# Attention's steps spread further, fill tokens found earlier, and three more tiles turned by transfers, in a fused attention and mixture-of-experts kernel

## Chip, cores, metric

One core of a Trainium2 chip. The time is device microseconds of one execution. The engines are TensorE (PE in the profile, with its weight loads PEld), VectorE (DVE), ScalarE (ACT), GpSimd (POOL) and SyncE (SP), which here only issues transfers.

## What is computed

The input is x, 8 sequences of 1024 tokens with 256 features. Everything is float32.

```python
xn = layernorm(x)
# causal linear attention, 16 heads of 16
q, k, v = xn @ Wq.T, xn @ Wk.T, xn @ Wv.T          # split into heads
q, k = elu(q) + 1, elu(k) + 1
out = einsum('blhd,blhde->blhe', q, cumsum(einsum('blhd,blhe->blhde', k, v), 1))
den = clip(einsum('blhd,blhd->blh', q, cumsum(k, 1)), 1e-6)
attn = (out / den).reshape(...) @ Wo.T
# mixture of 8 experts, the best 2 of each token
w, e = top_k(xn @ Wr + br, 2);  w = softmax(w)
ffn = sum over the 2 experts of w * ((silu(xn @ W1[e]) * (xn @ W3[e])) @ W2[e])
return x + attn + ffn
```

W1 and W3 are 256x512 for each expert, W2 is 512x256.

## The kernel before

**Two streams of work.** The 8192 tokens are 16 blocks of 512 for norm, router and attention. For the experts, each token appears twice; the 16,384 entries are sorted by expert and cut into rows of 128, called tiles here. There are room for 135 tiles (NF), of which 132 (NM) always run and 3 only if the counts ask for them. A first batch of 25 tiles (N1) comes from the first 4 blocks, so that expert work can begin early; a second list covers the rest and serves tiles 25 and up. `tile_step(j)` runs for j = 0 to 132: it carries tile j through the experts and puts beside it a piece of the other work: blocks 4 to 15 through norm, turn and router (j below 12), the making of the second list (j = 12 to 22, LISTS = 12, READ = 22), and steps of attention.

**A tile.** `ffn_load(j)` has POOL gather the tile's 128 rows of x (`xg`) and its entries of a small table (`entry`: router weight and the two numbers of the norm). `ffn_norm` (ACT) normalises the rows. PE needs them with features on partitions. Up to tile TURNED - 1 `ffn_turn` does that: two 128x128 transposes on PE into PSUM and a copy on ACT, all in step j - 1. From TURNED on, a transfer does it: `ffn_halves` (DVE) splits the float32 words into two planes of 16 bits, `ffn_turn_halves` has SP issue a transposing transfer between the loads of the tile's W1 and W3, and `ffn_join` (ACT) puts the planes together again in step j - 1. For this the norm comes in step j - 2, a step earlier than for a tile turned on PE. `ffn_hidden` makes gate and up (64 matmuls for the two, in `gu_ps`), silu on ACT and the product on DVE (`hT`); `ffn_out`, a step later, makes y (`y_ps`), scaled by the router weight on DVE; `ffn_store` has POOL add the rows to `out` (tiles 0 to 24: to a copy `acc_d`) with an indirect, adding transfer. Transfers that add to the same tensor wait for each other.

**Weights.** `ffn_weights(j + 2)` in step j has SP load 512 KB each of W1 and W3 into five buffers, so a load goes out when the matmuls five loads earlier are done. W2 stays resident.

**Attention's steps.** A block has 8 (`block_steps`): k, q, v; then scores of the first chunk, denominators (`den`, `over`) and their spreading over partitions by 8 transfers on SP (`rden`), and a load of the next block's turned x (`xnT`); then four chunks (`weigh` makes `oT`, `attend` multiplies by Wo into `a_ps` and copies to `at`), whose results POOL adds to `out` 256 KB at a time; the last block's go in one transfer of 512 KB (`n = NCH if t == NBLK - 1`). There are 129 steps (LAST), the last being only the final `attend`. `attend_upto` runs them up to a number `upto` that depends on j; 18 (AHEAD) are done after step 21.

**The second list.** `second_batch` is a generator, advanced by `piece(place)` at five places of a step, in steps 14 to 21 and once more at the start of step 22, and once at the end of step 12. Its first part computes counts and offsets; then 32 groups of one-hot matmuls (`held_ps`, from `at_place` on DVE and `parts` on ACT) add up, in `all_held`, which entry sits in each place. From that come `num_i` (which table row), `src_i` (which token to read) and `dst_i` (to which to add). Empty places must add their zeros to a token that no other row of the tile names; `other_tokens` finds one for each expert and partition (`fill`): a product `at_0_ps` on PE and nine operations on 128x8 elements on DVE. Then 15 operations on 128x110 turn `fill` into `fills`, place by place.

**What sets the order.** PE runs in program order. On the other engines a planner lays out the instructions at build time, in order of readiness and program order; those marked `in_order` are kept in place to a degree. Each engine then works through its queue in order.

The lines the change and the prediction touch: 764 to 787 (`second_batch`), 532 to 545 (`other_tokens`), 1476 (`TURNED`), 1523 (`piece`), 1584 (`upto`), 1312 to 1400 (a tile's load, halves, turns, weights), 1430 to 1447 (`ffn_out`, `ffn_store`), 1098 to 1117 (`attend`).

Of the kernel before, what the change touches and what calls it, by code (L numbers as in the profile page):

```python
# [64 lines left out]
def tile_attention_moe(  # L65
# [33 lines left out]
    NM = NF - NR  # L99
# [70 lines left out]
    for t in range(FB, FB + 2):  # L170
# [9 lines left out]
        fill=0.0, base=0, channel_multiplier=-1,  # L180
# [5 lines left out]
        fill=0.0, base=-1, channel_multiplier=-1,  # L186
# [8 lines left out]
        fill=0.0, base=0, channel_multiplier=1,  # L195
# [3 lines left out]
        fill=0.0, base=HD - 1, channel_multiplier=-1,  # L199
# [542 lines left out]
    def second_batch(taken):  # L742

        rows = sizes(True)
        left = f_one.tile([P, E], F32, name="left")
        nc.vector.tensor_tensor(left, rows, taken, ALU.subtract)
        upto = add_up(left, "upto2")
        past = past_experts(upto, N2, f_x, "xb")
        te, te_i = numbers_of(past, N2, "2")
        nc.vector.tensor_copy(rows_left, upto[0:1, E - 1 : E])  # L750

        room = f_one.tile([P, E - 1], F32, name="room2")
        nc.vector.tensor_scalar(
            room, rows[:, 0 : E - 1], -1.0, float(ROWS), ALU.mult, ALU.add
        )
        nc.vector.tensor_tensor(room, room, taken[:, 1:E], ALU.add)
        of_tiles = rows_of(past, past, room, taken[:, 0:1], N2, "rows2")
        in_row, place = places(NT)

        short = f_one.tile([P, E], F32, name="short")  # L760
        nc.vector.tensor_scalar(short, rows, 1.5, None, ALU.is_lt)
        num_i = const.tile([P, N2], I32, name="of2_i")
        all_held = f_one.tile([P, N2], F32, name="all_held")
        others = other_tokens(short)
        next(others)
        yield
        for j in range(2):
            for a in range(0, NT, 16):
                ps = ps_y.tile([P, 2, N2], F32, tag="y", name="held_ps")
                for b in range(a, a + 16, PART):  # L770
                    at, parts = one_hot(in_row, place, of_tiles, j, b, N2)
                    yield
                    for i in range(PART):
                        nc.tensor.matmul(
                            ps.rearrange("p w n -> p (w n)"), lhsT=at[:, i, :],
                            rhs=parts[:, i].rearrange("p w n -> p (w n)"),
                            start=(b + i == a), stop=(b + i == a + 15),
                        )
                for w in range(2):
                    if j == 0 and a == 0 and w == 0:  # L780
                        nc.vector.tensor_copy(all_held, ps[:, 0, :])
                    else:
                        nc.vector.tensor_tensor(all_held, ps[:, w, :], all_held, ALU.add)
                yield
        nc.vector.tensor_copy(num_i, all_held)
        _, src_i = tokens(all_held, N2, NT, "2_i")
        fill = next(others)
        fills = f_one.tile([P, N2], F32, name="fills")
        for e in range(E):
            mine = fills  # L790
            if e > 0:
                mine = f_two.tile([P, N2], F32, tag="mine", name="mine")
            nc.vector.tensor_scalar(
                mine, te, float(e), fill[:, e : e + 1], ALU.is_equal, ALU.mult
            )
            if e > 0:
                nc.vector.tensor_tensor(fills, fills, mine, ALU.add)
        empty = f_one.tile([P, N2], F32, tag="at_i", name="empty")
        nc.vector.tensor_scalar(empty, all_held, 0.5, None, ALU.is_lt)
        nc.vector.tensor_tensor(empty, empty, fills, ALU.mult)  # L800
        dst_i = const.tile([P, N2], I32, name="dst2_i")
        nc.vector.tensor_tensor(dst_i, src_i, empty, ALU.add)
        batches[1] = tab_d[1], te_i, num_i, src_i, out_rows, dst_i
        yield
# [346 lines left out]
    LAST = NBLK * STEPS + 1  # L1151
# [233 lines left out]
    def ffn_weights(j, halved=True):  # L1385
        e = expert_of(j, mybir.EngineType.SP)
        for s, w in enumerate((w1, w3)):
# [6 lines left out]
            )  # L1394
            if s == 0 and halved and j >= TURNED:
                ffn_turn_halves(j)
# [54 lines left out]
    def ffn_step(j, behind, between, after, late, finish):  # L1451
# [7 lines left out]
        if j < NM:  # L1459
            ffn_hidden(j, j == NM - 1, between)  # L1460
            after()
        if j + 1 < TURNED:
            ffn_turn(j + 1)
# [9 lines left out]
                stored[0] += 1  # L1473


    TURNED = 27
    gathered = ffn_load(0)
    with tc.issue_after(gathered.ins):
        in_order(nc.gpsimd.tensor_copy(te_late, batches[0][1]))
# [17 lines left out]
    LISTS = NBLK - FB  # L1497
    READ = LISTS + 10
    AHEAD = 2 + LISTS // 2 + READ - LISTS
# [12 lines left out]
    def tile_step(j):  # L1512
        nonlocal routing
        if j + 1 < TURNED:
            ffn_norm(j + 1)
        if TURNED <= j + 2 < NM:
            ffn_norm(j + 2)
            ffn_halves(j + 2)
        t = FB + j
        turning = 0 < j and t < NBLK  # L1520
        counting = FB < t <= NBLK and t % ROUND == 0

        def piece(place):
            if LISTS + 2 <= j < READ or (j, place) == (READ, 0):
                next(held["lists"])

        def of_routing():
            nonlocal routing
            if t <= NBLK:
                with tc.issue_after((last_token if j < 3 else last_masked)[0].ins):  # L1530
                    if "lgT" in held:
                        tp = ps_y.tile([P, P], F32, tag="y", name="lg_t")
                        nc.tensor.transpose(tp, held.pop("lgT"), ident)
                        add_logits(t - 1, 1, tp)
                    if routing and not counting:
                        for _ in routing:
                            pass
                        routing = None
                    if counting:
                        routing = route(t - ROUND, t)  # L1540
                        next(routing)
                    of_blocks = [] if j == 0 else [t + 1, t + 2] if j == 1 else [t + 2]
                    if not counting:
                        take_stats(of_blocks)

        def between():
            if not stepped and j > 0:
                of_routing()
            if turning:
                turn(t)  # L1550
            piece(2)

        def after():
            piece(3)

        def late():
            nonlocal waits
            if waits:
                attend_upto(waits)
                waits = None  # L1560

        def finish():
            if turning:
                held["lgT"] = f_two.tile([P, P], F32, tag="lgT", name="lgT")
                nc.scalar.copy(held["lgT"], logits(t))
            if counting:
                next(routing)
                with tc.issue_after(held_y[0].ins):
                    take_stats([t + 2])
            if t + 1 < NBLK:  # L1570
                normalise(t + 1)
            if turning and t + 5 < NBLK:
                load_x(t + 5, nc.scalar)

        if LISTS <= j < LISTS + NBLK - FB:
            rows = slice((t - LISTS) * TB, (t - LISTS + 1) * TB)
            in_order(nc.sync.dma_start(out=out_rows[rows, :], in_=x_rows[rows, :]))
        piece(0)
        if j < LISTS:
            upto = 3 + j // 2  # L1580
        elif j < READ:
            upto = AHEAD - (READ - j - 1)
        else:
            upto = AHEAD + (LAST - AHEAD) * (j - READ + 1) // (NM - 3 - READ)
        before_step = steps_made[0]
        waits = attend_upto(upto, put_off=True)
        stepped = steps_made[0] > before_step
        if stepped or j == 0:
            of_routing()
        piece(1)  # L1590
        ffn_step(j, LATE if N1 < j <= N1 + LATE else 0, between, after, late, finish)
        piece(4)
        if j == LISTS:
            for _ in routing:
                pass
            in_order(
                nc.sync.dma_start(
                    out=tab_d[1][1 : 1 + NS * P, :].rearrange("(p i) w -> p (i w)", p=P),
                    in_=tab.rearrange("p i w -> p (i w)"),
                )  # L1600
            )
            in_order(nc.sync.dma_start(out=tab_d[1][0:1, :], in_=before[0:1, 0:3]))
            held["lists"] = second_batch(taken)
            next(held["lists"])
        if j == N1 + 1:
            copied.append(j)
            in_order(nc.sync.dma_start(out=out_rows[0 : FT * P, :], in_=acc_d[:, :]))

    routing = None
    with tc.manual_schedule(engines={EN.PE}):  # L1610
        for j in range(NM + 1):
            tile_step(j)
# [54 lines left out]
```

## Time and profile before

Three runs took 1238.14, 1243.5 and 1246.43 us, median 1243.5. The profiled execution took 1239.72 us, its span (first to last instruction) 1238.0, at a mean granted clock of 0.995.

| | PE | PE weight load | DVE | ACT | POOL |
|---|---|---|---|---|---|
| busy us | 1193.1 | 1051.0 | 689.0 | 588.9 | 551.1 |
| share of the span | 96% | 85% | 56% | 48% | 45% |

| stage | us | PE busy | DMA share |
|---|---|---|---|
| first blocks, first list | 0 to 62 | 47.02 of 62 | 0.93 |
| second list, from tile 13 on | 155 to 279 | 118.97 of 124 | 0.66 |
| middle | 400 to 600 | 198.48 of 200 | 0.92 |
| middle | 800 to 1000 | 199.16 of 200 | 0.94 |
| last tiles | 1195 to 1225 | 28.23 of 30 | 0.65 |
| after PE | 1225 to 1238 | 0 | 0.18 |

The DMA share is the mean busy share of the 16 DMA engines. In a row of the timeline stand: start, duration, engine and line, operation, output and inputs with their shapes, how many in a row were merged, and in brackets how long the engine had been idle before and what ended that (the releaser, inferred from semaphores). SPq is SP's queue, where the duration is that of issuing, not of the transfer.

### The profile page before, as it was taken

To read this page: it belongs to the slowest core of one execution; us is meant where nothing else is said; L and a number is where in the kernel's file an instruction comes from. 1 tells how busy PE (TensorE), PEld (TensorE's weight loads), DVE (VectorE), ACT (ScalarE), POOL (GpSimd) and SP (SyncE) were. 2 spreads that over 40 slices of the span, in tenths; PEclk is the share of its full clock that TensorE was granted. 3 is DMA by queue.
4 is the path that set the end of the run, shared out by engine and by line. 5 is a ranking of instruction groups with operands and counts; after the bars stand their busy time and mean duration, and the time that the engine had idled before them with its cause. 6 is when DMAs were issued, how large, how long until landed. Compare 5 with 4: busy or idle time off the path is not lost. (4 is left out here: it accounts for less than half of the span.)

```text
span 1238.0 us, 29843 instructions
## 1 busy us (share of the span) xinstructions
PE 1193.1 (96%) x11394; PEld 1051.0 (85%) x11394; DVE 689.0 (56%) x1519; ACT 588.9 (48%) x1098; POOL 551.1 (45%) x473
## 2 busy tenths in 40 slices
PE   8799999999999999999999999999999999999995
PEld 6588887977889888989888898889898888889884
DVE  7766678765464545546464645454554646464541
ACT  5656576771543526262624445352627262534521
POOL 4734434334353645353455444454444544454422
PEclk9999999999999999999999999999999999999998
DMA  9888777657979899989999898899999988999884
GB/s 330 291 270 282 197 201 204 202 154 194 244 182 213 185 224 192 206 188 206 188 198 196 188 218 183 190 200 222 191 212 187 222 170 207 189 195 211 183 180 71
DMA packets 232446, 252.67 MB, mean 204 GB/s; under 512 B 101458, under 2 KB 156370, under 8 KB 232018
## 3 DMA queue, kind: packets, MB, share of 16 engines
q1 hardware_dynamic: 189298, 198.61, 58.8%
q0 software_dynamic: 38256, 43.22, 25.2%
q10 hardware_dynamic: 4752, 8.91, 2.0%
q8 instruction: 94, 1.54, 0.5%
q14 instruction: 46, 0.38, 0.1%
HBM read 187.91 MB, written 44.29 MB: 188 GB/s over the span
## 5 line engine op out<-in xcount | busy, mean ns | idle before, releaser
L1411 PE MATMUL gu_ps<-xgT,w 128*128 128x128 f32 x4224 | 506.2, 277 | 5.9 <-issue 3.0
L1411 PEld LDWEIGHTS gu_ps<-xgT,w 128*128 128x128 f32 x4224 | 490.6, 192 | 20.7 <-issue 12.0
L1443 POOL DMA_INDIRECT out_dram<-y,dst_i x107 | 175.6, 1641 | 330.6 <-DVE y L1437 52.8
L1430 PE MATMUL y_ps<-w_sb,hT 128*128 x1056 | 250.4, 380 | 1.3 <-DVE hT L1422 0.9
L1419 ACT ACTIVATE hT<-gu_ps 128x512 f32<-128x512 f32 x132 | 79.4, 602 | 291.4 <-PE gu_ps L1411 245.4
L1430 PEld LDWEIGHTS y_ps<-w_sb,hT 128*128 128x128 f32 x1056 | 190.5, 190 | 22.9 <-issue 1.2
L1025 DVE TENSOR_TENSOR s_sb<-s_ps,causal 128x512 f32<-128x512 f32 x256 | 162.0, 685 | 85.3 <-PE s_ps L1016 72.7
L1315 POOL DMA_INDIRECT xg<-in_x_dram,src_i x132 | 135.6, 1027 | 148.9 <-DVE half L1340 49.7
L1320 POOL DMA_INDIRECT entry<-tab_d,of_i x107 | 109.9, 1027 | 32.6 <-issue 32.0
L1422 DVE TENSOR_TENSOR hT<-gu_ps,hT 128x512 f32<-128x512 f32 x132 | 90.5, 685 | 48.5 <-PE gu_ps L1411 28.9
L1437 DVE TENSOR_SCALAR y<-y_ps,entry 128x256 f32<-128x256 f32 x132 | 63.6, 481 | 94.7 <-PE y_ps L1430 86.8
L1340 DVE COPY half<-xg 128x512 uint16<-128x512 uint16 x105 | 47.9, 456 | 109.0 <-ACT xg L1330 99.7
L1114 ACT COPY at<-a_ps 128x256 f32<-128x256 f32 x64 | 23.8, 371 | 173.0 <-PE a_ps L1109 156.8
L1358 ACT COPY xgT<-halfT 128x512 uint16<-128x512 uint16 x105 | 80.3, 765 | 3.5 <-DMA halfT<-half 1.9
L1330 ACT ACTIVATE xg<-xg,entry 128x256 f32<-128x256 f32 x132 | 79.0, 599 | 2.8 <-DMA xg<-in_x_dram,src_i 2.6
L1016 PE MATMUL s_ps<-qm,kT 32*128 32x256 f32 x1024 | 74.4, 400 | 0.6 <-DVE hT L1422 0.6
L1109 PE MATMUL a_ps<-wo_sb,oT 128*128 128x256 f32 x256 | 67.8, 387 | 4.9 <-DVE oT L1080 4.9
L1443 POOL DMA_INDIRECT acc_d<-y,src_i x25 | 42.7, 1709 | 65.0 <-DVE y L1437 20.0
L1063 PE MATMUL o_ps<-s_sb,va 128*32 128x128 f32 x2048 | 69.7, 276 | 0.2 <-issue 0.2
L1063 PEld LDWEIGHTS o_ps<-s_sb,va 128*32 128x32 f32 x2048 | 52.3, 109 | 18.3 <-issue 16.4
L1117 POOL DMA_DIRECT2D out_dram<-at x26 | 34.7, 1336 | 68.8 <-DMA out_dram<-y,dst_i 42.2
L1016 PEld LDWEIGHTS s_ps<-qm,kT 32*128 32x128 f32 x1024 | 47.0, 184 | 14.6 <-issue 7.4
(236 smaller groups left out, 1418.4 us busy)
## 6 DMA issues: line engine op xcount, KB each, us to landing
w<-in_w_dram SPq DMA_DIRECT2D x264, 512.0 KB
rden<-over SPq DMA_DIRECT2D x128, 64.0 KB
xnT<-xnT_d SPq DMA_DIRECT2D x15, 512.0 KB
out_dram<-at POOLq DMA_DIRECT2D x25, 256.0 KB
out_dram<-in_x_dram SPq DMA_DIRECT2D x12, 512.0 KB
xnT_d<-xnT ACTq DMA_DIRECT2D x11, 512.0 KB
xb<-in_x_dram SPq DMA_DIRECT2D x9, 512.0 KB
w_sb<-in_w_dram SPq DMA_DIRECT2D x4, 1024.0 KB
```

The lines of the kernel that those rows point to most:

```text
L1016: nc.tensor.matmul(s_ps[r][:, hh].rearrange("p a l -> p (a l)"), lhsT=kT[rows, hh, span], rhs=qm[rows, hh, :, span], start=True, stop=True,)
L1025: last_masked[0] = nc.vector.tensor_tensor(sm, s_ps[r].rearrange("p k a l -> p (k a) l"), causal_b, ALU.mult)
L1063: nc.tensor.matmul(o_ps[32 * r : 32 * r + 32, hh, :], lhsT=va[:, c, 4 * hh + r, a, :], rhs=s_sb[r][:, 2 * hh + a, :], start=(first and a = ...
L1315: rows = nc.gpsimd.indirect_dma_start(out=xg[j], out_offset=None, in_=x_rows[:, :], in_offset=bass.IndirectOffsetOnAxis(ap=src_i[:, i : i ...
L1320: of_rows = nc.gpsimd.indirect_dma_start(out=entry[j], out_offset=None, in_=table[:, :], in_offset=bass.IndirectOffsetOnAxis(ap=num_i[:, i ...
L1330: nc.scalar.activation(xg[j], xg[j], AF.Identity, bias=entry[j][:, 1:2], scale=entry[j][:, 2:3])
L1358: nc.scalar.copy(xgT[j].bitcast(U16).rearrange("p k (l b) -> p b k l", b=2), halves.pop(j).rearrange("p (b k) l -> p b k l", b=2),)
L1411: done = nc.tensor.matmul(ps[:, i, :], lhsT=w13[:, k, bass.ts(i, P)], rhs=xgT[j][:, k, :], start=(k == 0), stop=(k == KC - 1),)
L1419: silu = nc.scalar.activation(hT, gu[0], AF.Silu)
L1422: nc.vector.tensor_tensor(hT, gu[1], hT, ALU.mult)
L1430: done = nc.tensor.matmul(y_ps, lhsT=hT[:, i, :], rhs=w2_sb[:, bass.ds(e * (IC * H) + i * H, H)], start=(i == 0), stop=(i == IC - 1),)
L1443: nc.gpsimd.indirect_dma_start(out=rows[:, :], out_offset=bass.IndirectOffsetOnAxis(ap=dst_i[:, i : i + 1], axis=0), in_=ys.pop(j), in_off ...
```

## The change

Three edits.

1. Attention's steps after READ are spread so that the last come in step 130, not 128. (The words of the change speak of one last transfer; that it is one is so in the kernel before already.)
2. In `second_batch`, `fill` is asked for after its own new stop, in step 13 (`piece(1)`, after attention's step and ahead of the tile's gate and up matmuls), instead of behind the list in step 22. What turns it into `fills` stays.
3. TURNED goes from 27 to 24: the rows of tiles 24, 25 and 26 are turned by transfers.

```diff
         others = other_tokens(short)
         next(others)
         yield
+        fill = next(others)
+        yield
         for j in range(2):
...
         nc.vector.tensor_copy(num_i, all_held)
         _, src_i = tokens(all_held, N2, NT, "2_i")
-        fill = next(others)
         fills = f_one.tile([P, N2], F32, name="fills")
...
-    TURNED = 27
+    TURNED = 24
...
         def piece(place):
-            if LISTS + 2 <= j < READ or (j, place) == (READ, 0):
+            if LISTS + 2 <= j < READ or (j, place) in ((READ, 0), (LISTS + 1, 1)):
                 next(held["lists"])
...
-            upto = AHEAD + (LAST - AHEAD) * (j - READ + 1) // (NM - 3 - READ)
+            upto = AHEAD + (LAST - AHEAD) * (j - READ + 1) // (NM - 1 - READ)
```

## The prediction

> **What bounds the kernel now.** I read the share of busy time by stretches first, then the chain that ended last, then the timeline of the last 70 us and of 260 to 310 us, where the edits land.
>
> ```profile
> 600.00:800.00 200.00, 198.38 (x1904) 175.62 (x1903) 105.50 (x190) 89.07 (x146) 94.45 (x76) 1.00 0.92 199
> ...
> 1205.00:1215.00 10.00, 10.00 (x79) 9.67 (x78) 1.97 (x5) 2.50 (x4) 1.65 (x1) 1.00 1.00 205
> 1215.00:1225.00 10.00, 8.86 (x56) 7.72 (x54) 2.54 (x5) 0.60 (x1) 3.10 (x2) 1.00 0.31 36
> ```
>
> The columns are stretch, length, busy us of PE, weight load, DVE, ACT and POOL, granted clock, DMA share, GB/s. PE works 99% of the middle at full clock; no step of attention there waits for a free slot. So moving attention's steps between tiles can't shorten the middle. Only less PE work, a stall, or the end can change the time. The end is not PE's:
>
> ```profile
> 1197.42 1.56 POOL L1443 DMA_INDIRECT out_dram<-y,dst_i  x1 [7.44 <-DVE y L1437]
> 1201.76 1.40 POOL L1117 DMA_DIRECT2D out_dram<-at  x1 [2.78 <-ACT at L1114]
> 1212.07 1.65 POOL L1443 DMA_INDIRECT out_dram<-y,dst_i  x1 [8.92 <-DVE y L1437]
> 1216.68 1.55 POOL L1443 DMA_INDIRECT out_dram<-y,dst_i  x1 [2.96 <-issue]
> 1221.26 1.54 POOL L1443 DMA_INDIRECT out_dram<-y,dst_i  x1 [3.02 <-DVE y L1437]
> 1226.59 1.55 POOL L1443 DMA_INDIRECT out_dram<-y,dst_i  x1 [3.79 <-DVEq L1621]
> 1231.05 1.54 POOL L1443 DMA_INDIRECT out_dram<-y,dst_i  x1 [2.91 <-DMA out_dram<-y,dst_i]
> ```
>
> The stores of tiles 126 to 131, with attention's last transfer (512 KB) between the first two. All add to `out`, so each goes out when the one before has landed. The releaser in the third row is wrong: tile 127's y was there at 1206.49 (its DVE row: 1206.01 + 0.48), so it was the transfer that held the store back, 10.31 us after its own issue. From there four steps of 4.6, 4.6, 5.3 and 4.5 us lead to the last store, though PE ends at 1224.71 and tile 131's y at 1225.23. The end, 1238.0, is 6.95 us behind the last store's issue. The queue of stores is 5.8 us late (1231.05 against 1225.23).
>
> **The turns by transfer.** Three pairs like
>
> ```profile
> 285.10 0.38 PE L1368 MATMUL xg_t<-ident,xg 128*128 128x128 f32 x2
> ```
>
> leave PE: 3 x 0.38 = -1.14 us, all on the path, as PE is full. For it come three half copies on DVE (0.43 to 0.76), on ACT copies of 0.76 for 0.37, and three transposes on SP's queue (1.25 each). Norms of tiles 24 to 26 come a tile earlier. Tile 24's rows were asked for at 242.24, tile 25's at 274.32, just ahead of its norm at about 277; ACT then idles up to 281.72 (4.20 us), so a wait of a microsecond there is covered. With that cover gone it would cost that microsecond. The tight place is tile 25's transpose, because of SP's order:
>
> ```profile
> 284.23 7.09 SPq L997 DMA_DIRECT2D rden<-over  x8
> 291.36 0.67 SPq L830 DMA_DIRECT2D xnT<-xnT_d  x1
> 292.83 4.14 SPq L1390 DMA_DIRECT2D w<-in_w_dram  x5
> 297.10 1.64 SPq L1349 DMA_TRANSPOSE halfT<-half  x1
> ```
>
> The five loads are both of tiles 25 and 26 and the first of 27 (the row below them is tile 27's transpose). Tile 25's transpose would stand behind the first, at 293.3. What one takes in this traffic, a later place tells:
>
> ```profile
> 506.43 1.26 SPq L1349 DMA_TRANSPOSE halfT<-half  x1
> ...
> 513.85 0.77 ACT L1358 COPY xgT<-halfT 128x512 uint16<-128x512 uint16 x1 [0.58 <-DMA halfT<-half]
> ```
>
> 7.4 us to use; two other joins that waited give 7.0 (707.85 to 714.88) and 6.8 (1040.70 to 1047.47). So tile 25's join starts at 300.1 to 300.7 and ends 0.76 later. PE, rid of two turns, reaches its gate/up matmuls (300.79 now) at 300.03: a stall of 0.8 to 1.5, taken as 1.1. The other order: from block 3 on, where such transposes exist, SP has the loads and the transpose of the next tile but one ahead of rden (349.71 and 357.27 against 357.71). Then tile 25's goes out at about 279, nothing waits, and part of this stall of 1.38 us may go:
>
> ```profile
> 294.89 0.76 DVE L1340 COPY half<-xg 128x512 uint16<-128x512 uint16 x1 [0.91 <-ACT xg L1330]
> 295.57 0.47 DVE L1437 TENSOR_SCALAR y<-y_ps,entry 128x256 f32<-128x256 f32 x1
> 295.96 0.41 DVE L1080 TENSOR_TENSOR oT<-rden,o_ps 128x256 f32<-128x256 f32 x1
> 296.24 0.99 POOL L1320 DMA_INDIRECT entry<-tab_d,of_i  x1 [0.30 <-issue]
> ...
> 296.51 1.10 PE L1109 MATMUL a_ps<-wo_sb,oT 128*128 128x256 f32 x4 [1.38 <-DVE oT L1080]
> ```
>
> oT stands behind tile 27's half copy, which waits for a double norm that this change moves to tile 22. I take half of it, -0.7. Both orders being in this trace (285 and 357), I take the mean of +1.1 and -0.7: +0.2, with ends -1.38 and (see the slow rival) +6.8.
>
> A rule speaks against this part: the Trainium skill, "VectorE: DVE Perf Modes", section "The three transpose paths", has 390 ns on TensorE against 1309 ns by transfer for 128x128 in bf16 and advises TensorE where PSUM will do. The rows have the same order (0.38 for the pair against 7 us), but latency only counts where someone waits. From the page four blocks would be 5.2 us, an estimate; tile 25's join would end at 299.3 and the stall be nothing.
>
> **The fill tokens.** Their nine small DVE operations (L532 and L537 stay near 171 and 180; the seven of L539 to L545 sum to 1.28 us by their rows at 267.75 to 270.53) and one PE product go from tile 22 to tile 13. The product there waits for `at_0`, ready at 171.53 (L532: 171.08 + 0.45); PE would come to it at 172.02, so 0.5 us are left, and behind it tile 13's matmuls. DVE's extra 1.3 to 1.4 us delay the first one-hot: ACT has its parts at 180.28, PE takes them at 182.09, 1.8 us later. Both fit: 0, up to +1 if not. At tile 22 the product (0.15) goes and DVE gets 1.3 us back, but what follows on POOL is back to back behind a store (267.32 + 1.56, then entries at 269.19, 271.32, 272.62), so gathers gain nothing: 0. The 15 operations that make `fills` stay where they are.
>
> **The spread and the end.** 111 steps over tiles 22 to 130 instead of 128; each step has the same work, two still share the last tile. Tiles 129 and 130 get steps, 131 none. PE's total is unchanged. "One last transfer" is not new: the 512 KB one above is it. It moves by two tiles. Its issue trails the start of the gate/up matmuls that follow it by 1.25 us (1200.51, 1201.76), so behind tile 130's (1211.11 - 1.14 + 0.2 = 1210.17) it comes at 1211.42. Stores behind it: 129, 130, 131, three for five. How long it takes: in the 11 us from 1201 the POOL queue's packets took 30.3% of 16 engines (3.3 us), the loads' 57.5% (6.3 us); at 1211 no loads are left. A store of 128 KB takes 4.6 in the quiet; four times that, by 3/4 of 3.3 us more, 7.0. Ends: 10.31 as now, and no less than a store, 4.6. With 7.0: stores at 1218.4, 1223.0, 1227.6, end 1234.6. With 10.31: 1237.9. With 4.6: 1232.2. Tile 131's y, at 1224.3, holds none back.
>
> **Sum.** Span 1238.0 - 3.4 = 1234.6; of it -0.94 comes through PE, the rest from the queue of stores. The profiled execution took 1239.72, 3.8 below the median of 1243.5 shown; the same difference makes 1240.1.
>
> **Rivals.**
> 1. *Transfer as slow as now.* Its 10.31 us are the adding itself, not the loads beside it: 256 KB took 6.69 (356.20 to 362.89), 128 KB 4.6, and that grows much like 10.31 for 512. Against it: the 6.3 us of loads. End 1237.9, no gain: 1243.4.
> 2. *Slower: tile 25's join holds oT.* ACT is in order: the join at 300.7 (SP as at 284), then tile 27's norm (0.6), its half copy on DVE (0.76), and if oT still stands behind that copy, oT ends at about 303.2 instead of 296.37. PE waits 6.8 us more. With -1.14 and -2.3 from the end: +3.4, 1246.9; slower from a stall of 3.4 on. For it: today's order of the rows at 294.89 to 295.96. Against it: DVE's order isn't pinned there and is laid out anew, and block 3 shows the better order on SP.
> 3. *The spread does nothing, only the turns count*: if the queue of stores were not the bound, -0.94, 1242.6. The 5.8 us of lateness speak against it.
>
> **How the numbers follow.** Forecast 0.55; rivals 1 and 3 together 0.25; rival 2 0.15; something else that the new order of instructions brings 0.05. Range: from the quick transfer with the 1.38 stall gone (1232.2 - 1.6 = 1230.6, that is 1236.1) less some scatter of the runs (8.3 us from lowest to highest), 1234.5, to rival 2 with about 1 us, 1248. The likeliest case alone: 1236 to 1242. 1% (12.4 us) is about what a measurement of this kernel can tell from no change; no case above reaches it. Leaving 12% for what isn't in the list, more of it on the slow side, where the new waits are: faster by over 1% 0.04, within 0.88, slower 0.08.
>
> **What would show it.** The 512 KB transfer at about 1211 with three stores behind it, the first 7 us later: right; 10 us: rival 1. Six fewer 128x128 turns on PE (48). PE waits near 295 to 301, by oT or xgT: over 1.5 us is rival 2. A PE wait ahead of tile 13's matmuls at 172: the cover of `at_0` was too thin. Wrong would be any new idle time of PE between 400 and 1150 of more than 5 us in all, where I expect none.

## The result, and the profile after

The changed kernel takes 1249.67 us (median of 10 runs, 1247.31 to 1253.15), the kernel before 1238.49 on the same chip (median of 10, 1232.98 to 1246.43): a ratio of 1.0086, 95% interval [1.0058, 1.0114], slower by some 10.7 us. The forecast was 1240.1, with 1248 as the upper end. That the difference stays within 1% was right; its sign and size were not. (With ten executions the median of before lies 5 us under that of the three that the prediction started from, so the forecast is best read as 3.4 us less than before.)

The profiled execution of the changed kernel took 1253.09 us, its span 1251.0, that is 13.0 longer than the span of before, at a mean granted clock of 0.982 for 0.995. PE turns six blocks fewer and is still busy longer (1203.5 us for 1193.1). The stretches say where. After, first; then the two of before that differ (columns as in the prediction: stretch, length, busy us of PE, weight load, DVE, ACT, POOL, granted clock, DMA share, GB/s):

```profile
155.00:215.00 60.00, 55.12 (x454) 46.91 (x452) 51.11 (x136) 42.01 (x113) 24.88 (x18) 1.00 0.66 183
279.00:310.00 31.00, 24.96 (x210) 20.89 (x209) 11.90 (x21) 3.96 (x9) 15.64 (x14) 0.83 0.61 149
600.00:800.00 200.00, 198.28 (x1869) 175.71 (x1868) 103.05 (x188) 90.66 (x147) 96.15 (x77) 1.00 0.90 197
```

```profile
155.00:215.00 60.00, 56.75 (x477) 48.38 (x478) 48.84 (x116) 42.12 (x113) 25.59 (x19) 1.00 0.70 198
279.00:310.00 31.00, 28.53 (x345) 24.85 (x341) 16.09 (x29) 6.02 (x13) 14.22 (x13) 1.00 0.80 196
```

The middle is as it was (198.28 against 198.38). From 279 to 310 PE does 210 matmuls instead of 345, idle longer and at a lower clock; from 155 to 215, where the fill tokens went, it loses 1.6 us.

The start of each tile's gate/up matmuls, after less before, aligned at tile 14, puts a place to it: +2.03 at tile 15, +2.61 at 16, +4.17 at 17, +3.95 at 22, +4.92 at 23, **+12.28 at 24**, +9.98 at 32, +11.48 at 131.

**Tiles 15 to 17: the fill, and the clock.** PE waits for the one-hot parts of the second group, in the timeline of PE:

```profile
186.06 0.81 PE L776 MATMUL held_ps<-parts,at_place 128*128 128x220 bf16 x4 [1.30 <-ACT parts L627]
194.93 2.05 PE L1412 MATMUL gu_ps<-xgT,w 128*128 128x128 f32 x16 [0.46 <-DVE s_sb L1026]
```

The reason stands in DVE's queue. After:

```profile
179.49 0.61 DVE L620 TENSOR_TENSOR held<-rows,in_row 128x440 bf16<-128x440 f32 x1
...
180.09 1.28 DVE L898 TENSOR_TENSOR_SCAN ksum<-ones,upto_t,kT 128x512 f32<-128x512 f32 x1
...
184.52 1.14 DVE L620 TENSOR_TENSOR held<-rows,in_row 128x440 bf16<-128x440 f32 x2
```

Before, the second and third `held` came ahead of the scans of `ksum`:

```profile
179.76 0.60 DVE L620 TENSOR_TENSOR held<-rows,in_row 128x440 bf16<-128x440 f32 x1
...
180.37 0.60 DVE L620 TENSOR_TENSOR held<-rows,in_row 128x440 bf16<-128x440 f32 x1
180.89 2.44 DVE L897 TENSOR_TENSOR_SCAN ksum<-ones,upto_t,kT 128x512 f32<-128x512 f32 x2
```

The first group is 1.24 us late (179.49 against 178.25), and that is covered, as predicted. But the planner, with nine operations more in that stretch, put the scans ahead of the second group, which is 4.8 us late. The 15 operations of `fills` have moved too, from 271 to 276 before to 186 to 195 now, between the groups. Together this is the +2.61 of tile 16. The other 1.56 us at tile 17 come with the clock: it is granted by half for 3.41 us from 216.7 on, behind a wait of 2.87 us for `oT`. Before has that wait too (2.88 us), without the halved clock.

**Tile 23: a half copy.** The timeline over all engines:

```profile
282.55 0.95 POOL L1316 DMA_INDIRECT xg<-in_x_dram,src_i  x1 [0.30 <-issue]
283.71 0.60 ACT L1331 ACTIVATE xg<-xg,entry 128x256 f32<-128x256 f32 x1 [2.41 <-DMA xg<-in_x_dram,src_i]
...
284.34 0.65 DVE L1341 COPY half<-xg 128x512 uint16<-128x512 uint16 x1 [3.36 <-issue]
284.92 0.47 DVE L1438 TENSOR_SCALAR y<-y_ps,entry 128x256 f32<-128x256 f32 x1
...
285.97 0.69 DVE L1026 TENSOR_TENSOR s_sb<-s_ps,causal 128x512 f32<-128x512 f32 x1 [0.58 <-PE a_ps L1110]
...
286.76 1.60 PE L1412 MATMUL gu_ps<-xgT,w 128*128 128x128 f32 x10 [2.22 <-issue]
...
289.48 2.01 PE L1412 MATMUL gu_ps<-xgT,w 128*128 128x128 f32 x6 [1.13 <-issue]
291.75 0.29 DVE L990 TENSOR_SCALAR over<-den 128x128 f32<-128x128 f32 x1 [5.09 <-PE gu_ps L1412]
291.81 0.37 ACT L1115 COPY at<-a_ps 128x256 f32<-128x256 f32 x1 [7.50 <-PE gu_ps L1412]
291.96 1.88 DVE L1026 TENSOR_TENSOR s_sb<-s_ps,causal 128x512 f32<-128x512 f32 x3
...
292.74 3.75 PE L1412 MATMUL gu_ps<-xgT,w 128*128 128x128 f32 x16 [1.24 <-PE gu_ps L1412]
```

ACT waits for the gather of tile 25 and normalises at 283.71. DVE's next instruction in the queue is that tile's half copy, so DVE idles 3.36 us, and behind it stand y and the masks of the scores (`s_sb`; the first was at 280.67 before). The scores fill the four PSUM buffers that `gu_ps` uses too: PE begins tile 23 0.10 us after the first mask ends (285.97 + 0.69), 2.22 us idle, and its second half 0.10 us after the second (291.96 + 0.68, the first of the three in the row). Before, the mask waited for no copy, and the row of tile 23 shows no idle time (timeline, all engines):

```profile
280.67 0.68 DVE L1025 TENSOR_TENSOR s_sb<-s_ps,causal 128x512 f32<-128x512 f32 x1
...
281.52 3.74 PE L1411 MATMUL gu_ps<-xgT,w 128*128 128x128 f32 x32
```

The granted clock halves for 10.24 us from 288.4 on: the 16 matmuls at 292.74 take 3.75 us for the usual 1.95. From tile 22 to tile 24 all this makes 8.3 us, of which 4.6 are idle time in PE's rows. Not all of it is explained by the half copy: `over` on DVE waits 5.09 us, and `at` on ACT 7.50, and both start only at 291.8, although PE's `den` and `a_ps`, which they read, are over by 284.6 according to PE's rows, whose ends are modelled. The 1.13 us of idle time within tile 23's first half has no visible cause either. What held them is open.

**The end.** POOL's rows, as the prediction read them:

```profile
1210.80 1.55 POOL L1444 DMA_INDIRECT out_dram<-y,dst_i  x1 [6.58 <-DVE y L1438]
1219.82 1.55 POOL L1444 DMA_INDIRECT out_dram<-y,dst_i  x1 [7.46 <-DVE y L1438]
1224.03 1.35 POOL L1118 DMA_DIRECT2D out_dram<-at  x1 [2.66 <-ACT at L1115]
1231.53 1.64 POOL L1444 DMA_INDIRECT out_dram<-y,dst_i  x1 [6.15 <-DMA out_dram<-at]
1236.23 1.55 POOL L1444 DMA_INDIRECT out_dram<-y,dst_i  x1 [3.06 <-DMA out_dram<-y,dst_i]
1240.83 1.55 POOL L1444 DMA_INDIRECT out_dram<-y,dst_i  x1 [3.04 <-DMA out_dram<-y,dst_i]
```

The 512 KB transfer has three stores behind it, the first 7.50 us later, and the last goes out 3.79 us behind tile 131's y (5.82 before). But from the last store to the end of the span it is 10.17 us now (6.95 before). So the 13.0 us are +11.8 in PE's stream (the start of tile 131, not aligned), -2.0 in the stores, +3.2 behind them.

### The profile page after: what moved, and what is told of

Read it like the earlier page. It is cut to its first block, busy times and chain, and to the rows that moved or that the text cites. A ratio compares the mean times of both kernels' runs of the same rounds, so it can differ in the third digit from the quotient of the medians.

```text
span 1251.0 us, 29839 instructions
## 1 busy us (share of the span) xinstructions
PE 1203.5 (96%) x11388; PEld 1058.2 (85%) x11388; DVE 689.9 (55%) x1522; ACT 588.3 (47%) x1098; POOL 551.9 (44%) x473
## 3 DMA queue, kind: packets, MB, share of 16 engines
q8 instruction: 94, 1.54, 0.5%
## 4 chain that ended last, share of the span: by engine, by line
PE 87%; DVE 5%; DMA 3%; issue 2%; ACT 2%; another core or an unknown queue 0%; POOL 0%; POOLq 0%; ACTq 0%; DVEq 0%
PE gu_ps L1412 37%; PE y_ps L1431 17%; PE s_ps L1017 5%; PE o_ps L1064 5%; PE a_ps L1110 5%; PE zkk L866 4%; PE zkv L866 4%; PE zq L845 4%; PE o_ps L1046 2%; PE tp L357 1%; PE o_ps L1074 1%; PE den L983 1%; DMA out_dram<-y,dst_i 1%; DMA wr_sb<-in_wr_dram 1%; PE lg_ps L375 1%
## 5 line engine op out<-in xcount | busy, mean ns | idle before, releaser
L1444 POOL DMA_INDIRECT out_dram<-y,dst_i x107 | 178.7, 1670 | 345.9 <-DMA out_dram<-y,dst_i 52.5
```

The costliest lines, as they stand in the source:

```text
L1444: nc.gpsimd.indirect_dma_start(out=rows[:, :], out_offset=bass.IndirectOffsetOnAxis(ap=dst_i[:, i : i + 1], axis=0), in_=ys.pop(j), in_off ...
```

## The experiments

They ran on four other chips, on which the kernel before took 1221.8 to 1222.7 us; each is compared with before on its own chip. Changes are to the kernel before unless said. "Held" means that instructions are kept behind others on their engine (`issue_after`). The time is the median of 5 to 12 executions, and the ratio comes with its 95% interval; it is not the quotient of the two medians and differs from it by up to 0.14% (1.7 us).

| kernel | us | ratio to before, 95% |
|---|---|---|
| spread alone | 1221.58 | 0.9988 [0.9971, 1.0005] |
| fill alone | 1223.27 | 1.0011 [0.9997, 1.0025] |
| fill, `fills` held | 1222.28 | 0.9997 [0.9979, 1.0014] |
| fill amid the list, `fills` held | 1223.12 | 1.0007 [0.9993, 1.0022] |
| turns alone | 1228.45 | 1.0051 [1.0033, 1.0068] |
| turns, half copies held | 1224.53 | 1.0026 [1.0008, 1.0045] |
| spread, fill with `fills` held | 1225.17 | 1.0016 [0.9999, 1.0032] |
| fill and turns | 1231.7 | 1.0067 [1.0046, 1.0088] |
| spread and turns | 1230.03 | 1.0076 [1.0050, 1.0102] |
| spread and turns, half copies held | 1225.89 | 1.0021 [0.9999, 1.0044] |
| the same with pads | 1225.36 | 1.0016 [0.9997, 1.0034] |
| the changed kernel | 1230.56 | 1.0078 [1.0054, 1.0101] |
| the changed kernel with pads | 1231.71 | 1.0068 [1.0043, 1.0094] |
| changed, `fills` and one half copy held | 1229.88 | 1.0048 [1.0032, 1.0063] |
| before, again | 1222.21 | 1.0010 [0.9990, 1.0031] |

And the starts of tiles on these chips in the profiled executions, less those of the kernel before (profiled on one of them), aligned at tile 14:

```
tile   spread  fill   fill amid  turns  turns held  spread+turns  same, held  changed
 15     0.00   2.02     0.00     0.00      0.00        0.00          0.01      2.02
 17    -1.60   2.61    -1.61    -1.61      0.01       -0.05          0.01      2.38
 20    -1.61   2.61    -0.16    -1.61      0.01       -0.05          0.01      2.38
 22    -1.61   2.41    -0.35     2.13      0.01        3.72          0.01      2.19
 23    -1.61   2.41    -0.36     2.13      0.17        3.72          0.17      3.92
 24    -1.61   2.41    -0.35     1.92     -0.05        3.50         -0.05      3.78
 28    -1.63   2.38    -0.38     2.25     -0.26        2.92          0.21      3.81
 30    -1.46   2.38    -0.38     2.25     -0.26        3.19          1.99      5.84
 32    -1.21   2.08    -0.18     1.19     -1.54        3.48          2.32      6.08
```

The -1.6 at tile 17 are no effect of an edit: in that execution of before the clock halved for 3.41 us there, behind the wait of 2.87 us for `oT`, which is in every kernel. It did so in 12 of the 17 profiles, with and without the fill. Nor are the rises of "same, held" and "changed" between tiles 28 and 30: PE waits 1.33 and 1.58 us there for the `xgT` of tile 29, and in the same two kernels with pads it does not (+0.00 each).

**One part at a time.**

```diff
-            upto = AHEAD + (LAST - AHEAD) * (j - READ + 1) // (NM - 3 - READ)
+            upto = AHEAD + (LAST - AHEAD) * (j - READ + 1) // (NM - 1 - READ)
```

> Before with one edit: attention's steps spread to tile 130. Theory P (the three parts add up, and the loss comes from the other two): the 512 KB transfer goes out about 1211 with three stores behind it, the first of them 7.5 us later, and the last store follows 3.8 us behind tile 131's y instead of 5.8; time 2 to 3 us under before, no new wait of PE. Rival R (the spread itself costs: the last stretch, with 10.2 us from the last store to the end in the changed kernel's profile against 7.0, takes back what the queue of stores gives): no gain, 0 to 3 us slower, and the long end is seen again here.

The last store is 4.80 us behind y, the end 7.0 behind it, no new wait of PE: theory P's signs, and not rival R's long end. By the ratio the gain is 1.5 us, with an interval from -3.5 to +0.6. The mechanism is there, its worth can't be told from nothing.

```diff
+        fill = next(others)
+        yield
         for j in range(2):
...
-            if LISTS + 2 <= j < READ or (j, place) == (READ, 0):
+            if LISTS + 2 <= j < READ or (j, place) in ((READ, 0), (LISTS + 1, 1)):
...
-        fill = next(others)
         fills = f_one.tile([P, N2], F32, name="fills")
```

> Before with one edit: the fill tokens found at tile 13. Theory P: the 15 operations that make `fills` go out on DVE in tiles 14 and 15 between the one-hot products that PE waits for; PE is idle some 2 us more between 180 and 210, tile 17's gate/up matmuls start 3 to 4.5 us later than before, and the time is 2 to 4.5 us over before. Rival Q (what was seen there is the clock, which halves in one execution and not in another, whatever the edit): the start of tile 17 within 1 us of before once the clock's stretches are taken off, time within 1 us of before.

The same two waits as in the changed kernel, in the timeline of PE:

```profile
178.54 0.81 PE L776 MATMUL held_ps<-parts,at_place 128*128 128x220 bf16 x4 [1.29 <-ACT parts L627]
...
187.41 2.05 PE L1412 MATMUL gu_ps<-xgT,w 128*128 128x128 f32 x16 [0.46 <-DVE s_sb L1026]
```

So the fill brings them, with no turn or spread beside it: 2.02 us at tile 15, 2.6 by tile 16. Of this the time shows 1.3 us by the ratio, from -0.4 to +3.1: less than theory P's 2 to 4.5, and not clear of nothing.

```diff
-    TURNED = 27
+    TURNED = 24
```

> Before with one edit: tiles 24 to 26 turned by transfers. Theory P: tile 25's half copy stands ahead of the scores' masks on DVE, gu_ps of tile 23 finds no free PSUM buffer, PE is idle 3 to 5 us between 284 and 295 and the clock halves behind it; tile 24's gate/up matmuls start 6 to 9 us later than before; time 5 to 8 us over before. Rival Q (the halved clock was a chance of that one execution, or needs the delay that the fill part brings): tile 24 starts at most 3 us later, time from 1 us under to 2 us over before.

As dear as theory P said (6.2 us by the ratio), but not at the place it named. The wait is a tile earlier, behind tile 24's half copy (timeline, all engines):

```profile
259.66 0.81 PE L774 MATMUL held_ps<-parts,at_place 128*128 128x220 bf16 x4 [1.49 <-ACT parts L627]
...
260.32 1.09 ACT L1330 ACTIVATE xg<-xg,entry 128x256 f32<-128x256 f32 x2
261.44 0.43 DVE L1340 COPY half<-xg 128x512 uint16<-128x512 uint16 x1 [1.84 <-ACT xg L1330]
261.78 0.48 DVE L1437 TENSOR_SCALAR y<-y_ps,entry 128x256 f32<-128x256 f32 x1
...
262.32 0.60 PE L535 MATMUL at_ps<-at,ones 128*128 128x8 f32 x2 [1.85 <-DVE y L1437]
```

The copy waits for its norm, y stands behind it, and the fill product (here still at tile 22) needs the PSUM buffer that y frees. The norm itself waits for no gather here: ACT's rows show no idle time from 249.57 on, and the norms of tiles 23 and 24 come one after the other. PE's 1.85 us follow another wait of 1.49, for the last one-hot parts, which is in every kernel. The clock halves behind it: +3.74 at tile 22 against the run with the spread alone, whose clock did not halve at tile 17 either.

```diff
+        with tc.issue_after(last_token[0].ins):
             fills = f_one.tile([P, N2], F32, name="fills")
             for e in range(E):
...
```

> The fill part as in the run before it, but the 15 operations that make `fills` held behind the list, at tile 22, where they stand in the kernel before; the nine small operations and the product stay at tile 13. Theory P: it is the 15 operations that cost; PE's waits of tiles 14 to 17 are as before, time within 1 us of before. Rival S (the nine small operations are enough to delay the one-hot chain): tile 17 still starts 2 us or more later and the time is 2 us or more over before.

Mixed. The wait at tile 15 is the same (1.29 for the parts, +1.94), so the nine small operations are enough, as S says; only the 0.6 us of tile 16 are gone. Yet the time is that of before within 2 us, as theory P has it. What PE loses there doesn't reach the time whole; why not was not found.

**Together.** The changed kernel as it is, the fill with the turns, the changed kernel with `fills` held and tile 25's half copy behind `last_masked`, and the spread with the held fill:

> The changed kernel as it is, on the chip of the runs below. Theory P (the parts add): spread -1.5, fill +1.5 and turns +6.7, as the single edits gave beside before, so 6 to 7 us over before. Theory I (interaction: with the fill product gone from tile 22 PE comes to tile 23 earlier against tile 25's gather, so the half copy that stands ahead of the scores' masks waits longer than in the run with the turns alone): 9 to 13 us over before, PE idle 3 to 5 us in front of and within tile 23's gate/up matmuls, and the clock halved there.

> Before with two edits, the fill tokens at tile 13 and the turns of tiles 24 to 26 by transfers, without the spread. Theory I: PE is idle in tile 23 as in the changed kernel, 10 us or more over before, over the 8 us of the two single edits' sum. Theory P: 7 to 8.5 us over before. If the spread is what brings the loss in the changed kernel, 7 us or less here and clearly more there.

> The changed kernel with two orders mended: the 15 operations that make `fills` held behind the list, and tile 25's half copy held behind the scores' masks of tile 22. Theory I or P as to the half copy: no idle time of PE in tile 23, tile 24's gate/up matmuls start as in before within 2 us, the time 6 us or more under the changed kernel and from 2 us under to 2 us over before. Rival Q (the half copy's place is not it; any kernel with these turns loses): 4 us or more over before.

> Before with the spread to tile 130 and the fill product at tile 13, `fills` held behind the list; no turns changed. If the two parts add as the single edits did (-0.2 and +0.5): from 3 us under to 1 us over before. If the early product at tile 13 costs by itself (rival S): 2 us or more over the run with the spread alone.

The changed kernel is slower by 0.78% here, as on the first chip, and the half copy of tile 25 is again what PE waits for in tile 23:

```profile
276.23 0.60 ACT L1331 ACTIVATE xg<-xg,entry 128x256 f32<-128x256 f32 x1 [3.45 <-DMA xg<-in_x_dram,src_i]
276.86 0.43 DVE L1341 COPY half<-xg 128x512 uint16<-128x512 uint16 x1 [3.91 <-ACT xg L1331]
...
277.60 0.68 DVE L1026 TENSOR_TENSOR s_sb<-s_ps,causal 128x512 f32<-128x512 f32 x1
278.38 3.81 PE L1412 MATMUL gu_ps<-xgT,w 128*128 128x128 f32 x32 [1.57 <-issue]
```

Again `gu_ps` starts 0.10 us after the mask. This time the clock did not halve there and PE had no further idle time in tile 23: 1.6 us from tile 22 to tile 24, not 8.3. So the time, 9.5 us over before by the ratio and 8.3 by the medians, is theory I's rather than P's, but the trace shows neither the 3 to 5 us of idle time nor the halved clock that theory I named. The half-mended kernel missed its expectation: 3.7 us better than the changed one by the ratios (0.30%, with an interval of 3.4 us either way) and 0.7 by the medians, not 6; its last store was 9.5 us late and its end 10.2 long. No wait for a mask is left in its tile 23, but `hT` now stands behind the 15 held operations, PE waits 0.59 us for it, and tiles 22 to 24 still lose 1.1 us. Fill and turns without the spread lose 0.67%, 8.2 us, within theory P's range; but PE waits 2.14 us for tile 25's copy in tile 23, and the clock halves behind it, as theory I has it. The spread with the held fill lies 0.28% over the spread alone (on another chip), on the side of theory S. Theory I's amount fell with the next runs: without the fill, spread and turns lose as much. There the wait is in tile 22, behind tile 24's copy; with the fill product gone from that tile it is in tile 23, behind tile 25's.

**Where the half copies stand.** Before again, the fill amid the list, the turns with both half copies held, and spread with turns:

> The kernel before, with nothing edited, for a profile on the chip of these runs and a measure of the scatter: time within 2 us of before. Theory P (what the changed kernel lost between tiles 14 and 24 are waits that the edits brought): no wait of PE for the parts at tile 15 and none in tile 23, and the last store 5 to 6 us behind tile 131's y. If this profile shows the same waits, or the halved clock near tile 17, the edits are not what brought them.

> The fill part with its nine small operations and its product in the midst of the list (after the first half of the second round of sums, tile 18) in place of tile 13, `fills` held behind the list. Theory S (the nine operations at tile 13 delay the one-hot chain that PE waits for at tile 15): no wait for the parts at tile 15, tile 17 starts as in the run with the spread alone within 0.5 us of the same start at tile 14, time within 1 us of before. If the place doesn't matter: 1.3 us of waiting shows at another tile and tile 22 starts 2 us or more later.

```diff
-            ffn_halves(j + 2)
+            if j + 2 not in (N1 - 1, N1):
+                ffn_halves(j + 2)
...
+        if j + 2 == N1 - 1:
+            with tc.issue_after(last_token[0].ins):
+                ffn_halves(j + 2)
+        if j + 2 == N1:
+            with tc.issue_after(last_masked[0].ins):
+                ffn_halves(j + 2)
```

> The turns alone, with the half copies of tile 24 and of tile 25 held behind the list and behind the scores' masks, so that nothing that PE waits for stands behind them on DVE. Theory H (the half copies' place on DVE is what the turns cost): no wait at tile 22 (1.85 with the turns alone) and none at tile 23, tile 26 starts 1 us earlier than with no turns, time from 2 us under to 1 us over before. Theory B (the cost is that the queue of stores, once late, stays late: mean 9.9 us behind y with the turns alone against 4.5 to 8 without, and 9.7 against 5 at the last tile): time still 3 us or more over before, with the last store 8 us or more behind y.

> The spread and the turns without the fill part. The long end (10.1 us from the last store to the end of the span in three profiles of kernels with spread and turns, 7.0 in all others): if it belongs to spread and turns together, it is here and the time is 7 us or more over before; if it needs the fill part too, 7.0 here and 4 to 6 us over before, as with the turns alone.

Before shows no wait at tile 15 or 23, but its last store is 9.49 us late: that figure, 5.82 on the first chip, differs between executions of one kernel. The fill amid the list has no wait at tile 15; its product waits 0.97 us for y, which frees a PSUM buffer, at tile 19 instead: +1.45 at tile 20 against the spread alone. So the place decides which wait appears, as theory S has it; neither of the two places tried is without one. With the turns alone and both copies held, y, product and copy stand so (timeline, all engines):

```profile
261.68 0.48 DVE L1437 TENSOR_SCALAR y<-y_ps,entry 128x256 f32<-128x256 f32 x1
...
262.46 0.30 PE L535 MATMUL at_ps<-at,ones 128*128 128x8 f32 x2
...
269.07 0.41 DVE L1340 COPY half<-xg 128x512 uint16<-128x512 uint16 x1
```

No wait of the product for y, and +0.01 at tile 22. The loss falls from 0.51% to 0.26%, that is by 3.1 us with an interval of 3.1 either way. The turns' saving, forecast as 1.14 us, is 0.26 by tile 28. The reason stands in the profile of before from the same chip (timeline of PE):

```profile
278.07 0.38 PE L1368 MATMUL xg_t<-ident,xg 128*128 128x128 f32 x2
278.29 1.89 PE L1430 MATMUL y_ps<-w_sb,hT 128*128 x8
```

A pair is 0.38 us long, but the next matmul starts 0.22 behind its start: the rest overlaps. Three pairs are 0.66, and PE waits 0.30 for tile 25's join. (The 1.28 us that this kernel gains between tiles 30 and 31 are not the turns': that step takes from 8.0 to 9.8 us in these profiles whatever the edit, 8.05 in before on the first chip.) What is left of the loss, 3.2 us by the ratio and 2.7 by the medians, shows nowhere in that profile: its span is 2.1 us under that of before, whose profiled execution took 4.0 us more than its median. So theory H has its waits right and its time wrong. Theory B's signs, 3 us over and the last store 8.2 late, are met here; but before itself, unedited, had its last store 9.5 late. The rest of the loss stays open. Spread and turns without the fill lose 0.76%, and the end is long: the last store and the end are 10.1 us apart (1215.46 to 1225.6), against 7.0 in before.

**The long end, and the copies with the spread.** Six memsets of one column on POOL at the very start (the pads); the held copies with the spread; both.

> The changed kernel with six small memsets more on POOL at the very start, where nothing waits for them, so that POOL's last instructions stand six places later in its stream. If the long end is a matter of that place: 7.0 us from the last store to the end in place of 10.1, and 5 to 7 us over before in place of 8 to 9. If it belongs to spread and turns: 10.1 as before, 8 to 10 us over before.

> Spread and turns, the half copies of tiles 24 and 25 held behind the list and behind the scores' masks, no fill part. Theory H (the half copies' place): no wait of PE at tile 22 or 23; the turns' saving of 1.1 us and the spread's 1 us are there; with the long end (POOL's last instructions should stand at about 789) 2 to 4 us over before, with a short one 1 us under to 1 us over. Theory B (the stores' lateness): 6 us or more over before, the last store 8 us behind y.

> The kernel of the run before it with the six small memsets at POOL's start. If the place in POOL's stream makes the end long: 7.0 us from the last store to the end, and 3 us under the kernel without them, 2 us under to 1 us over before, the best of all kernels with the turns. If not: the same time as without.

The pads do nothing: the end is 10.1 us in both kernels that have them. The place in POOL's stream is refuted also by counting: the wait at the end of POOL's queue (a DRAIN) is the 775th of POOL's instructions in the trace in four profiles where it is long (4.12 us) and in six where it is short (1.54 to 1.58). That wait makes 2.5 of the 3.1 us, the instruction ahead of it (1.19 for 0.57) the rest. Of 17 profiles, the seven with both spread and turns have 10.1 to 10.2 us, the ten others 6.9 to 7.0. That it goes with the pair is shown; why is not.

Holding the two copies takes spread and turns from 0.76% to 0.21%, as theory H has it (2.6 us over before, with the long end); theory B's 6 us and late last store do not come (4.3 late). That is 6.7 us by the ratios, with an interval of 4.2 either way, and 5.0 by the medians, on two chips. The two profiles account for 3.6 of it, at tile 24: the wait of 1.85 us and the halved clock. In the stretch around tiles 21 to 24, without and with:

```profile
255.00:300.00 45.00, 40.50 (x384) 34.97 (x383) 27.04 (x71) 16.55 (x37) 20.74 (x17) 0.96 0.64 162
```

```profile
255.00:300.00 45.00, 41.81 (x399) 36.28 (x398) 27.49 (x73) 18.09 (x39) 22.89 (x19) 1.00 0.72 181
```

PE is busy 1.3 us more and keeps its clock. The held kernels still miss the gain; no kernel here beats the one before by more than can be measured. The changed kernel itself, with fill, was not run with both copies held and nothing else moved.

## Why the prediction was wrong

On the first chip the span was forecast at 1234.6 us and became 1251.0. Of the 16.4 us between, 12.7 are PE's (11.8 late at tile 131 instead of 0.94 early), 3.2 the end behind the last store and 0.5 the last store's lateness. PE's 11.8 are, in order, 0.3 ahead of tile 14, 2.6 of the fill, 1.6 of the halved clock at tile 17, 8.3 from tile 22 to tile 24, and -1.0 for all the rest.

An account by the ratios on the other chips, on 1222 us: spread and turns with the copies held, +2.6, of which the long end alone is 3.1 (so the two intended savings come to half a microsecond); the place of the two copies, +6.7 (0.0076 less 0.0021); the fill on top, +0.2 (0.0078 less 0.0076). The sum, 9.5, is the changed kernel's loss by construction. Each step has an interval of 3 to 4 us either way, and the kernels ran on three chips.

- **The middle** (no gain, no loss): right, PE is busy 198.28 of 200, and between 400 and 1150 us it idles 4.4 us, for 4.3 before.
- **The turns, -1.14 on PE**: mis-sized. Duration was taken for occupancy: a pair takes 0.22 us of PE's time, not 0.38, so 0.66 in all, and 0.26 of it is left by tile 28 even with the copies held. (The advice to use TensorE that the prediction quotes beside the two figures is stated by the Trainium skill, "VectorE: DVE Perf Modes", in the section "Rules for kernel authors"; no kernel here with the three turns by transfer was faster.)
- **Tile 25's handover, +0.2 between -1.38 and +6.8**: this is the step that failed; it became +8.3 on the first chip (1.6 to 4.4 from tile 22 to 24 in the changed kernel's other two profiles). Both prices were for tile 25's own data, its join ahead of tile 25 or a copy ahead of `oT` at tile 24. The copies were counted as work off the path (0.43 to 0.76 on DVE) and the norm's wait as one of ACT's alone, covered by 4.20 us of idle time. But a copy on DVE waits in its queue for that norm (tile 24's is late because ACT is busy, tile 25's because of its gather), and what stands behind it is y and the masks of the scores; PE needs these for a PSUM buffer, two tiles before the rows are used. The held kernels show it: with both copies behind, neither wait is there. Rival 2 had the right sort of mechanism, a half copy that holds DVE, with the price of 6.8 us, at the wrong place and with a chance of 0.15. The argument against it, that DVE's order is laid out anew, was the argument for it: an order laid out anew is an order not seen.
- **The halved clock**: not in the forecast. On the first chip it is part of the 8.3 us; with the pads, 2.95 us of wait and a halved clock make 4.4 from tile 22 to 24. The Trainium skill, "TensorE: Matmul & The Clock Gate", section "Part 1: The HAM clock gate (the "warmup" mystery)", has the clock fall to half after an idle window of about 3.4 us, and the window free-running. The halved stretches in these traces are multiples of 3.41 us until PE's work ends, which agrees, and that the same wait of 2.87 us halves it in 12 profiles and not in 5 fits a free-running window; but less than a whole window was enough here: one wait of 2.14 us (fill and turns), and with the turns 1.49 and 1.85 us with 0.81 of work between them. One wait of 1.57 us was not.
- **The fill, 0 up to +1**: wrong in the profile, 2.0 to 2.6 us. The slack of the first one-hot group was read rightly; the second group's was not looked at, and the order of DVE behind it was taken as fixed. "The 15 operations that make `fills` stay where they are" was wrong too: the program text keeps them, the planner does not. The time of the kernels with the fill alone shows -0.4 to +1.3 us of it by the ratios, with intervals of 1.7 to 2.1 either way.
- **The end, -3.4** (with the turns): the transfer is right (7.50 us against 7.0, three stores behind). With the spread it took 7.0 to 7.9 us in nine profiles, without it, beside the loads, 7.9 to 10.4 in eight, which speaks against rival 1. The stores are 3.79 us late against a forecast of 3.3. "The end, 6.95 us behind the last store's issue" was carried over and became 10.17. And the start value, 5.8 us late, was one execution's: another of the same kernel has 9.5. That the end is longer with spread and turns was not expected by any rival, and its cause is open.

## What to carry to other kernels

Where a planner lays out the queues, an added instruction is to be priced by what ends up behind it, not by its duration; the new order is fixed when the program is built, so it can be compared with the old one, engine by engine, before any time is forecast. A small operation that waits for a transfer or for a busy engine belongs behind everything that the bounding engine waits for on that queue; holding two copies back so was worth 6.7 us of 1222 with the spread and 3.1 without it, each by the ratios and give or take 3 to 4. What an instruction frees on TensorE here is nearer the distance from its start to the next one's than its duration, and a stall of two microseconds there is to be priced with the chance of a halved clock behind it.

## What was not expected of the hardware

- The long end: with spread and turns together the stretch behind the last store is 3.1 us longer, in seven profiles of seven on four chips, though the last stores follow each other as elsewhere (4.4 to 4.7 us apart).
- The kernel before takes 1238.5 us on one chip and 1221.8 to 1222.7 on four others. Of the difference between two profiled executions 10.1 us lie between tiles 14 and 131, spread over many stretches; the cause was not looked for.
- The queue of adding stores stays late for hundreds of microseconds: averaged over tiles 30 to 119, 4.2 us behind y in one profile of before and 8.3 in another, up to 15.7 in the half-mended kernel. Where it was measured it cost PE little: between 400 and 1150 us PE's idle time is at most 0.6 us in the 15 profiles of the four chips. At the last tile it moves the end.
